# Two shared down products moved behind the turns of the last two dense tiles

## The chip, the cores and the metric

The kernel runs on one core of one Trainium2 chip. Its time is the device time of one execution in microseconds; the time before is the median of three runs. One further execution was recorded by the hardware profiler; all durations below come from it.

The engines are called by their profile names: PE is TensorE (matrix products), PEld its weight loads, DVE is VectorE, ACT is ScalarE, POOL is GpSimd and SP is SyncE. They run at the same time and wait for each other through semaphores; each works through its own instructions in order.

## The reference, cut to what matters

The input is eight batches of 256 rows with 512 columns. The model adds a cross attention to x, and then a mixture of experts:

```python
x = x + xattn(layernorm(x), ctx, mask, Wq, bq, Wk, bk, Wv, bv)
flat = layernorm(x)                      # 2048 tokens of 512
g = flat @ shared_gate.T                 # 352 wide
u = flat @ shared_up.T
shared_out = sigmoid(g) * u @ shared_down.T          # float32
weights = softmax(flat @ router_w.T)                 # 8 experts
comb = the two largest weights of each token, 0 elsewhere
he = sigmoid(xb @ wg) * (xb @ wu)        # bfloat16, each expert
routed = sum over experts of comb * (he @ wd)
x = x + layernorm(x) + shared_out + routed
```

What is computed for a token therefore has a shared part (float32) and the part of its two experts (bfloat16).

## The kernel before, in words

**Attention first.** The first three quarters of the span and more are the attention of the eight batches, head by head. The change does not touch it.

**The tokens of all but the last half batch are sorted by expert.** They go through the experts in `NT` = 37 tiles of 128 rows, whose results are scattered to DRAM (`zs`) and read back later. The last half batch (batch 7, rows 128 to 255) can't be sorted in time. Its 128 tokens go through all eight experts, one tile for each: these are the *dense tiles*, numbers 37 to 44. Their results are summed in one PSUM bank called `sum`.

**Three steps for each tile**, made by `stream`:
- `gate_up_of(t)` (L820): gate product `eg` and up product `eu`, four matmuls each; ScalarE takes the tanh (L825), VectorE multiplies it into h, the tile `hz` (L826).
- `turn_h(t)`: h is turned by three matmuls into the bank `pht` (L836 for a dense tile, where the weight of the expert is multiplied in by a diagonal matrix); for a dense tile ScalarE copies it to SBUF as `hT` (L841).
- `down_of(t)` (L849): three matmuls of hT with the down weights; a dense tile's go to `sum`.

The stream is software-pipelined: after `gate_up_of(t)` stand `down_of(t-2)` and `turn_h(t-1)`. So a gate and up product usually stands between the turn of a tile and its down product. At the stream's end there are no more tiles to put there; its last five steps are down 42, turn 43, down 43, turn 44 and down 44.

**The shared part of the last batch** comes from `shared_units(B - 1, False)`: 24 fine steps (gate and up, L940; h by L952 and L964) and six down products (L998), each a float32 product of 128 columns of h with 512 columns of `sdT`, three chunks for each half of the batch. The chunks of the second half (`tt` = 1, elements 27 to 29 of the list) go into the bank `sum`, on top of the dense tiles' results. Those of the first half (`tt` = 0, elements 24 to 26) go into a bank `psy`, behind two matmuls (L997) that merge the expert results of that half. VectorE then adds the residual: L1012 for `sum`, with the output on SyncE's queue (L1016); L1007 for `psy`, in two parts of 256 columns, with outputs on the queues of SyncE and ScalarE (L1010).

**The order at the end is written out by hand.** The list `todo` (L1303) is gone through in order, and each step issues its instructions at once. `by(n, steps)` makes one step of n. Between the steps the loop issues `adds`: VectorE's additions of read-back expert results to the other halves (L917), each pair followed by its output on SyncE's queue (L919). `done` sums the steps' costs, an addition is issued when `done` passes `due`, and all that are left are issued from some step near the end on.

Of the kernel before, what the change touches and what calls it, by code (L numbers as in the profile page):

```python
# [36 lines left out]
def xattn_ffn_kernel(  # L37
# [840 lines left out]
    def give_back():  # L878


        halves = [(b, tt) for b in range(B) for tt in range(2)][:NS]
        room = deque(
            [four.tile([P, T], F32, tag=tag, name="again") for tag in "qk" for _ in range(3)]
        )
        for _ in range(3):
            e = three.tile([P, 2, T], F32, tag="e", name="again2")
            room.extend(e[:, i, :] for i in range(2))
        byrow = zs.rearrange("(r c) t -> r c t", c=2)
        Z = []

        def rooms(pool, tag, n, tiles=1):

            for _ in range(tiles):
                z = pool.tile([P, n, 2, T], BF16, tag=tag, name="z_" + tag)
                Z.extend(z[:, j] for j in range(n))

        def all_rooms():
            rooms(two, "V", 3, 2)
            rooms(three, "extra", 1, 3)
            rooms(two, "xT", 2)  # L900
            rooms(two, "x", 2)
            rooms(five, "acc", 1)
            rooms(one, "O", 1)

        def again(b, tt):
            S[b]["acc", tt] = a = room.popleft()
            nc.gpsimd.dma_start(out=a, in_=ACC[b][tt])

        def results(n):
            if not Z:  # L910
                all_rooms()
            nc.sync.dma_start(out=Z[n], in_=byrow[n * P : (n + 1) * P])

        def add(n, c):
            b, tt = halves[n]
            a = S[b]["acc", tt]
            nc.vector.tensor_add(a, a, Z[n][:, c, :])  # L917
            if c == 1:
                nc.sync.dma_start(out=out[b, tt * P : (tt + 1) * P, :], in_=a)  # L919

        n = range(NS)
        return (
            deque(lambda of=of: again(*of) for of in halves[: 2 * (NB - 1)]),
            deque(lambda i=i: results(i) for i in n), deque(lambda i=i, c=c: add(i, c) for i in n[:-1] for c in range(2)),
            lambda c: Z[NS - 1][:, c, :],
        )
# [257 lines left out]
    for b in range(B):  # L1184
# [15 lines left out]
        elif b == B - 1:  # L1200
# [5 lines left out]
            fetch, whom, experts, weighted, tiles = expert_tiles()  # L1206
# [57 lines left out]
    tiles, units = deque(tiles), deque(units)  # L1264
# [21 lines left out]
    again, results, adds, own_results = give_back()  # L1286
    n = 2
    while n <= NT:
# [7 lines left out]
    todo = shared_units(B - 1, False)  # L1296
    by = lambda n, todo: [
        (sum(us for us, _ in todo[i : i + n]), lambda fs=todo[i : i + n]: [f() for _, f in fs])
        for i in range(0, len(todo), n)
    ]  # L1300

    tiles = list(tiles)
    todo = tiles[:3] + by(4, todo[:24]) + tiles[3:] + by(3, todo[27:]) + by(3, todo[24:27])  # L1303
    done, due = 0.0, 7.0
    ring.remove(0)
    for i, (us, go) in enumerate(todo):
        go()
        done += us
        if i == 0:
            while results:  # L1310
                results.popleft()()
        while adds and (done > due or i >= len(todo) - 3):
            due += 0.5 if i < 9 else 1.0
            adds.popleft()()

# [32 lines left out]
```

## Time and profile before

| | us |
|---|---|
| median of three runs | 870.91 (870.66 to 870.98) |
| the profiled execution, whole time | 869.63 |
| its span | 867.8 |
| PE busy | 826.3 (95%) |
| DVE busy | 580.8 (67%) |
| turn of tile 43, its first matmul | starts 855.16 |
| last product into `psy`, end | 864.15 |

The page of the profile gives the busy time of each engine and its share of the span. The chain of waits follows the work that ended last back to its releasers; each of its rows has a start in us from the span's start, a length, and an engine with a tile and a line, and "xN" is the number of instructions in the row. "issue" is time for which the profile shows no cause; a row of DVEq or ACTq is that engine's hand-over. A timeline row has start, length, engine, line, operation, output<-inputs, shapes, and in brackets the idle time before it with what ended it. A length of several matmuls overlaps with the next row's, as matmuls are pipelined and their ends are modelled.

### The profile page before, as it was taken

Reading aid. Unit: us, or ns where it says so; the run is one execution under the profiler, and the core shown is the slowest. Engines: PE = TensorE matmul, PEld = TensorE weight load, DVE = VectorE, ACT = ScalarE, POOL = GpSimd, SP = SyncE. Lnnn points to the kernel's source line nnn. Section 1 sums busy time; section 2 is a strip of 40 time slices with the busy share of each in tenths; the row PEclk is TensorE's granted clock in tenths of the full one; section 3 lists DMA queues with packets and bytes.
Section 4 is the critical chain, followed back from the end, with each engine's and each line's share of the span. In section 5 each row is a group of like instructions: output and inputs, shape, how many; then the busy total and the mean of one; then the engine's idle time right before and its main releaser. Section 6 shows DMA issues by size and latency. Waiting matters only on the chain.

```text
span 867.8 us, 13410 instructions
## 1 busy us (share of the span) xinstructions
PE 826.3 (95%) x4987; PEld 340.0 (39%) x4987; DVE 580.8 (67%) x1106; ACT 365.6 (42%) x478; POOL 312.6 (36%) x380
## 2 busy tenths in 40 slices
PE   7988989999999999999999999999999989899997
PEld 4322323333333334333433343433343333455573
DVE  7666767776777677867676778676766674543347
ACT  4234444343344334433443343434343445256632
POOL 3114303543354345343525151605251223155520
PEclk9999999999999999999999999999999999999999
DMA  4107962231551257115712350011000000267556
GB/s 159 46 33 239 342 192 78 34 45 43 128 100 30 41 123 122 23 36 123 128 22 42 90 99 1 26 34 52 1 25 13 13 13 25 61 147 170 150 169 242
DMA packets 91973, 75.05 MB, mean 86 GB/s; under 512 B 60321, under 2 KB 77756, under 8 KB 91526
## 3 DMA queue, kind: packets, MB, share of 16 engines
q1 hardware_dynamic: 85302, 53.84, 22.8%
q0 software_dynamic: 5904, 19.70, 10.8%
q8 instruction: 40, 0.66, 0.3%
q10 hardware_dynamic: 704, 0.66, 0.2%
q14 instruction: 23, 0.19, 0.1%
HBM read 37.84 MB, written 40.79 MB: 91 GB/s over the span
## 4 chain that ended last, share of the span: by engine, by line
PE 74%; DVE 19%; issue 3%; POOL 2%; ACT 1%; DMA 0%; DVEq 0%; ACTq 0%; POOLq 0%
PE s L436 24%; DVE nm L438 10%; PE av L474 9%; PE psy L998 5%; PE pu L940 4%; PE psq L411 3%; PE psk L411 3%; PE ey L849 3%; PE eu L820 3%; PE eg L820 3%; PE pgu L940 3%; PE pg L940 3%; DVE q L418 2%; PE s L459 2%; PE psv L378 2%
## 5 line engine op out<-in xcount | busy, mean ns | idle before, releaser
L461 ACT ACTIVATE e<-s 128x1024 f32<-128x1024 f32 x256 | 262.0, 1023 | 398.5 <-PE s L459 396.6
L438 DVE TENSOR_REDUCE nm<-s 128x2 f32<-128x1024 f32 x256 | 313.3, 1224 | 144.4 <-PE s L459 131.3
L436 PE MATMUL s<-k,q 32*128 32x512 f32 x1024 | 287.7, 639 | 25.3 <-DVE nm L438 22.7
L459 PE MATMUL s<-q,k 32*128 32x512 f32 x1024 | 288.5, 640 | 1.5 <-DVE q L448 0.8
L474 PE MATMUL av<-e,V 128*32 128x512 f32 x1024 | 137.4, 605 | 0.2 <-ACT e L461 0.2
L436 PEld LDWEIGHTS s<-k,q 32*128 32x128 f32 x1024 | 76.6, 183 | 130.2 <-DVE nm L438 104.7
L401 POOL TENSOR_SCALAR extra<-mb,alpha,beta 128x512 f32<-128x512 f32 x60 | 45.5, 763 | 146.1 <-DVE q L418 145.7
L343 POOL TENSOR_TENSOR rs<-ve,mhalf 128x1 f32<-128x1 f32 x32 | 18.4, 575 | 217.0 <-DVE ve L341 216.9
L459 PEld LDWEIGHTS s<-q,k 32*128 32x128 f32 x1024 | 76.5, 182 | 5.3 <-issue 4.3
L474 PEld LDWEIGHTS av<-e,V 128*32 128x32 f32 x1024 | 20.3, 108 | 98.2 <-issue 96.3
L195 POOL DMA_INDIRECT xs<-xnb,at x30 | 30.2, 1006 | 73.9 <-DVE at L669 59.3
L826 DVE SCALAR_TENSOR_TENSOR hz<-eth,eu 128x352 bf16<-128x352 f32 x45 | 23.4, 520 | 41.6 <-ACT eth L825 18.2
L998 PE MATMUL psy<-sdT,h 128*128 128x512 f32 (+1 forms) x90 | 45.3, 615 | 0.2 <-issue 0.2
L940 PE MATMUL pu<-xT,sguT 128*128 128x256 f32 x128 | 36.7, 403 | 0.0
L940 PE MATMUL pg<-xT,sguT 128*128 128x256 f32 x128 | 35.3, 401 | 0.0
L378 PE MATMUL psv<-WvT,ctx 128*128 128x256 f32 x128 | 34.8, 394 | 0.0
L940 PE MATMUL pgu<-xT,sguT 128*96 128x256 f32 (+1 forms) x128 | 34.1, 393 | 0.0
L820 PEld LDWEIGHTS <-late_ctx 128*128 128x128 bf16 x296 | 27.6, 98 | 14.0 <-issue 2.6
L411 PE MATMUL psq<-xm,WqT 128*128 128x512 f32 x64 | 32.0, 620 | 0.9 <-DVE xm L1103 0.9
L195 POOL DMA_INDIRECT whose<-who,at x30 | 29.0, 968 | 9.1 <-issue 9.1
L940 PEld LDWEIGHTS pu<-xT,sguT 128*128 128x128 f32 x128 | 21.8, 189 | 25.3 <-issue 22.8
L411 PE MATMUL psk<-ctx,WkT 128*128 128x512 f32 x64 | 31.6, 617 | 0.0
(219 smaller groups left out, 980.4 us busy)
## 6 DMA issues: line engine op xcount, KB each, us to landing
xs<-blank SPq DMA_DIRECT2D x7, 1920.0 KB
x<-in_x_dram SPq DMA_DIRECT2D x7, 512.0 KB
ctx<-in_ctx_dram SPq DMA_DIRECT2D x7, 512.0 KB
accd<-acc SPq DMA_DIRECT2D x12, 256.0 KB
again<-accd POOLq DMA_DIRECT2D x12, 256.0 KB
out_dram<-again SPq DMA_DIRECT2D x12, 256.0 KB
gu<-in_L_ffn_w_gate_dram POOLq DMA_DIRECT2D x8, 352.0 KB
gu<-in_L_ffn_w_up_dram POOLq DMA_DIRECT2D x8, 352.0 KB
```

What stands on the lines that cost most here:

```text
L195: i = nc.gpsimd.indirect_dma_start(to[:, :], bass.IndirectOffsetOnAxis(ap=rows, axis=0), what, None, **bounds).ins
L378: nc.tensor.matmul(ps, ct[:, kc, sc * P : (sc + 1) * P], WvT[:, kc, :], start=(kc == 0), stop=(kc == 1))
L401: engine.tensor_scalar(t, S[b]["mb"], at, be, ALU.mult, ALU.add)
L411: nc.tensor.matmul(ps, W[:, kc, g // 2].rearrange("p j a d -> p (j a d)"), rhs[:, kc, :], start=(kc == 0), stop=(kc == 1),)
L436: nc.tensor.matmul(ps[:, jj, :], q[r, tci * P : (tci + 1) * P], k[r, :], start=True, stop=True)
L438: best = lambda: nc.vector.reduce_max(NM[G % 2][:, tci, c0 : c0 + 33 : 32], ps, axis=AX.X)
L459: nc.tensor.matmul(ps[:, jj, :], k[r, sc * P : (sc + 1) * P], q[r, :], start=True, stop=True)
L461: nc.scalar.activation(e, ps, AF.Exp)
L474: nc.tensor.matmul(AVT[G][32 * j : 32 * j + 32, :], V[:, sc, 2 * g + j // 2, j % 2 : j % 2 + 2, :].rearrange("p o d -> p (o d)"), et[j // ...
L820: nc.tensor.matmul(ps, xT[:, kc, :], weights_of(t, GU, I, (m * NKC + kc) * I), start=(kc == 0), stop=(kc == NKC - 1),)
L940: lambda kc=kc: nc.tensor.matmul(ps, sguT[:, m, kc, i0 : i0 + n + more], s["xT"][:, kc, :], start=(kc == 0), stop=(kc == NKC - 1))
L998: nc.tensor.matmul(t["y"], t["h"][:n, ic, tt * P : (tt + 1) * P], sdT[:n, ic, :], start=(ic == 0 and b < B - 1), stop=(ic == 2),)
```

## The change

The three products of the second half no longer stand together behind the stream. The first stands between the turn of tile 43 and its down product, the second between the turn of tile 44 and its down product, and the third behind the last down product, where all three stood. All three remain in the bank `sum`, which is read after the third. They are now three single steps instead of one, so the list has two steps more, and the loop's rule for the remaining additions counts four steps from the end instead of three.

```diff
     tiles = list(tiles)
-    todo = tiles[:3] + by(4, todo[:24]) + tiles[3:] + by(3, todo[27:]) + by(3, todo[24:27])
+
+    todo = (
+        tiles[:3] + by(4, todo[:24]) + tiles[3:-3] + todo[27:28] + tiles[-3:-1] + todo[28:29] + tiles[-1:]
+        + todo[29:] + by(3, todo[24:27])
+    )
     done, due = 0.0, 7.0
     ring.remove(0)
     for i, (us, go) in enumerate(todo):
@@
-        while adds and (done > due or i >= len(todo) - 3):
+        while adds and (done > due or i >= len(todo) - 4):
             due += 0.5 if i < 9 else 1.0
             adds.popleft()()
```

## The prediction

> **What bounds the kernel now.** I read the page first, then the chain of waits for the last 90 us, then the timelines of single engines over the last 15 us, because the change touches nothing earlier. The page says that TensorE is the busy engine over the whole span, at the full granted clock in every slice:
>
> ```profile
> PE 826.3 (95%) x4987; PEld 340.0 (39%) x4987; DVE 580.8 (67%) x1106; ACT 365.6 (42%) x478; POOL 312.6 (36%) x380
> PEclk9999999999999999999999999999999999999999
> ```
>
> That average says nothing of the last 13 us. The chain that ended last, in order of time (start, length, what), does:
>
> ```profile
> 854.68 0.65 PE sum L849 x3
> 855.33 0.18 PE pht L836 x3
> 855.51 0.02 issue
> 855.53 0.02 ACTq L841
> 855.54 0.04 issue
> 855.58 0.49 ACT hT L841
> 856.07 0.05 issue
> 856.12 0.82 PE sum L849 x3
> 856.94 0.18 PE pht L836 x3
> ...
> 857.73 0.82 PE sum L849 x3
> 858.55 2.58 PE sum L998 x6
> 861.13 0.43 PE psy L997 x2
> 861.56 2.59 PE psy L998 x6
> 864.15 0.02 issue
> 864.18 0.42 DVE acc L1007
> ```
>
> Read it so. Tile 42's down product (sum L849) still runs straight on from the work before it and costs 0.65 us for three matmuls. Behind it tile 43's h is turned (pht, 855.33) and TensorE has nothing else to do: it stands until ScalarE has copied the turned h to hT. The copy is on the path (0.49 us and 0.13 us of hand-over around it). Its down product then costs 0.82 instead of 0.65 us, since the first matmul behind a standstill also shows its own fill. The same happens once more with tile 44 (856.94 to 858.55). Then come the shared down products of the last half batch, three into the bank `sum` (858.55, two records for each float32 product, 2.58 / 3 = 0.86 us per product), two merging matmuls, three products into `psy`, and VectorE's last multiply-add. So in the tail TensorE sets the end, and two standstills on ScalarE's copy lie on that path.
>
> Two other engines could take the end over. VectorE's timeline:
>
> ```profile
> 856.07 0.52 DVE L826 SCALAR_TENSOR_TENSOR hz<-eth,eu 128x352 bf16<-128x352 f32 x1
> ...
> 859.76 1.41 DVE L917 TENSOR_TENSOR acc<-acc,z_acc 128x512 f32<-128x512 f32 x2
> 861.17 0.69 DVE L1012 SCALAR_TENSOR_TENSOR acc<-sum,acc 128x512 f32<-128x512 f32 x1
> 864.18 0.76 DVE L1007 SCALAR_TENSOR_TENSOR acc<-psy,acc 128x256 f32<-128x256 f32 x2 [2.32 <-PE psy L998]
> ```
>
> VectorE is full of adds until 861.17, takes `sum` there, is done at 861.86 and then idles 2.32 us for TensorE. SyncE's queue:
>
> ```profile
> 861.89 0.33 SPq L1016 DMA_DIRECT2D out_dram<-acc  x1
> 864.63 0.33 SPq L1010 DMA_DIRECT2D out_dram<-acc  x1
> ```
>
> The output of the half taken from `sum` is issued at 861.89; its data move from about 862.0 to 863.5 by the DMA view of these last us. The last output's data move from 865.2.
>
> **The change, part by part.** It removes no instruction and adds none: the built order has the same 4186 TensorE instructions, two products of L998 standing earlier, and on VectorE, ScalarE, GpSimd and SyncE the same order with the same waits. So the adds, although their rule (`done > due`, and the flush at the end) was touched, stay in the same order, and no DMA is moved past any other. Nothing queues behind a new wait: the weight load of hT already waits for ScalarE; it now has a product ahead of it.
>
> *First product, between tile 43's turn and its down product.* In place of the standstill TensorE runs 0.86 us, from 855.51 to 856.37. Meanwhile ScalarE copies as before: it is released by the turn's last matmul, which stands ahead of the product in both orders, so hT is ready at 856.12, 0.25 us before the product ends. Tile 43's down product then follows without standing: 0.65 us, to 857.02.
>
> *Second product, between tile 44's turn and its down product.* The turn costs 0.17, to 857.19; its h (hz) is on VectorE until 856.07 + 0.52 = 856.59, so it is in time by 0.4 us. Product to 858.05; hT ready at 857.19 + 0.61 = 857.80, again 0.25 us early; down product 0.65, to 858.70.
>
> *What is left.* One product into `sum` 0.86, to 859.56; the merging matmuls 0.43; three products 2.58: TensorE ends at 862.57 instead of 864.15. The saving is 1.58 us. Crosscheck from the other side: each standstill is 0.61 us plus the 0.17 us of the slower first matmul, 0.78; twice, 1.56.
>
> *What the two insertions may cost.* Each puts a float32 weight load straight behind a matmul of 128 columns and again a bfloat16 load behind float32 work. The second kind is free in the trace: the merging pair's bfloat16 loads lie under float32 matmuls (860.54 against a matmul that ends later) and that pair costs its plain 0.43. For the first kind the nearest row is the end of tile 38's turn:
>
> ```profile
> 834.47 0.33 PE L836 MATMUL pht<-diag,hz 128*128 128x128 bf16 x3
> 834.63 0.62 PE L940 MATMUL pgu<-xT,sguT 128*96 128x256 f32 x2
> ```
>
> Three turns start at 834.47 and the float32 matmul starts 0.16 us later, so no stall shows at its start; in the chain the sixteen matmuls of that group take 3.48 against 3.45 and 3.47 of the two groups behind it, so 0.00 to 0.03 us. [...] The row agrees that these loads are slow: 190 ns at L998 against 98 ns for bfloat16. If the load had to be complete before its matmul starts, all but the 57 ns of the turn's last matmul (0.17 / 3) would be bare, 0.13 us at each place, and the saving would be 1.58 - 0.27 = 1.31. [...] The row gives 1.52 to 1.58. I take 0.015 us each, by the row, since it is the same transition in the same queue, and keep 0 and 0.27 as ends: saving 1.55.
>
> *Where the stall goes.* Nothing new is late on TensorE. At the end, VectorE's last multiply-add can start at 862.60; VectorE is free from 861.86, so 0.74 us of cover is left there (it was 2.32). If VectorE were late by more than that, the saving would shrink by the excess. `sum` is complete at 859.56 instead of 861.13, but VectorE takes it at 861.17 as before, behind its adds: that earlier readiness is worth nothing. The last output is issued at about 863.07, when SyncE is past L1016 (862.22), and its data would move from 863.65, just behind the other half's, which end at 863.5; should they overlap, the bound is the rest of 128 KB, about 0.35 us at the 386 GB/s shown there. I count 0 for it.
>
> *Sum.* Profiled execution: 869.63 us, 867.8 of span and 1.8 around it; less 1.55 gives a span of about 866.25 and 868.1 us. The median of the runs shown is 870.91, 1.28 above that execution. Only the tail moves, so the difference carries over: 870.91 - 1.55 = 869.36, a saving of 0.18%.
>
> **The rivals.**
>
> *The wait stays, only behind the product.* If ScalarE saw the turn only when the product had passed (or hT's weight load couldn't go ahead during it), each standstill would still come after the 0.86 us, and the time would be 870.9 to 871.0 (with 0.06 for transitions). Against it: tiles 40 to 42 do the same thing with gate products in place of the shared one, and there ScalarE starts its copy while TensorE runs on (849.50, 851.57, 853.58, each with the copy at 0.48 us and no idle time ahead of the next down product). One covered and one bare would give 870.1.
>
> *The end passes to VectorE or to the output.* If the adds slipped by 1.5 us, the last multiply-add would start at 863.4 and the saving would be about 0.8: 870.1. For it: the adds read results that arrive late in the same stretch. Against it: no wait for data stands in that part of VectorE's timeline.
>
> *Slower than before.* The stretch from 855.5 to 862.6 becomes seven us of TensorE without a pause, two thirds of it float32. If the granted clock fell there, its 7.06 us would stretch. At half the clock that is 7.06 more, net 5.5 slower: 876.4. To end 0.2% slower it must eat 1.55 + 1.74 = 3.3 us, which needs a clock of 7.06 / 10.36 = 0.68. Against it: 834.80 to 845.20 is ten us of unbroken float32 at a granted clock of 1.00.
>
> *A little more than reckoned.* Two bfloat16 groups may start better than their steady 0.65, or runs scatter in its favour; beyond 1.74 us it counts as faster.
>
> **How the numbers follow.** About 0.2% (1.74 us) is what a measurement of this kernel can tell from no change, and my saving lies just inside. Full saving as worked out: 0.80; wait stays in full or half: 0.09; end passes to another engine: 0.06; slower clock: 0.05. Of the first, saving 1.55 with ends 1.31 and 1.6 and a scatter of some tenths between medians (the three runs differ by 0.32), about three in eight would be read beyond 1.74: 0.30 faster. Same takes the rest of it, 0.50, and both middle cases but 0.01: 0.64. Slower: 0.06. Range: low 868.4, which is nearly the profiled execution's own basis (868.1), since a set of runs may lie as low as that one did; high 870.6, which takes in half the saving and a scatter of 0.5. The likeliest case alone is 869.1 to 869.7.
>
> **What would show it.** In the changed profile: two records of L998 on `sum` directly behind each of the last two turns; no wait of TensorE for ScalarE's hT there, and down products of 0.65 us; ScalarE's copies at about 855.6 and 857.25; the last `psy` product ending near 862.6; VectorE's idle time ahead of L1007 down from 2.32 to about 0.75. Wrong would be: a wait for hT that remains behind the product, float32 loads that stand bare by over 0.1 us, VectorE ending its adds later than 861.2, or the last output landing less than 1.5 us earlier though TensorE ended so.

## The result and the profile after

The changed kernel's median is 869.01 us (867.94 to 869.90, 11 runs) against 870.91 (869.33 to 872.91, 11 runs); the ratio is 0.9977 with a 95% interval of 0.9967 to 0.9986. In a second comparison, on one chip, it was 869.43 us (22 runs) against 871.26 (61 runs), ratio 0.9982, interval 0.9972 to 0.9992. The ratios are not the quotients of the medians (869.43 / 871.26 is 0.9979). The first is 0.23% faster, the second 0.18%, which is the forecast; both intervals hold both values, so on which side of 0.2% the change lies is not settled.

The profiled execution of the changed kernel took 869.90 us with a span of 868.1, no less than the 867.8 of before. It came to the tail later, so spans say nothing here, and the tail has to be read for itself. This is its chain of waits, in order of time (start, length, what):

```profile
856.44 0.65 PE sum L849 x3
857.09 0.17 PE pht L836 x3
857.26 0.91 PE sum L998 x2
858.17 0.65 PE sum L849 x3
858.82 0.17 PE pht L836 x3
858.99 0.91 PE sum L998 x2
859.90 0.65 PE sum L849 x3
860.55 0.86 PE sum L998 x2
861.41 0.43 PE psy L997 x2
861.84 2.59 PE psy L998 x6
864.43 0.02 issue
864.46 0.42 DVE acc L1007
```

Both rows of ScalarE's copy have gone from the chain. Each turn (pht) is followed at once by a float32 product into `sum`, and the down products behind them are back at 0.65 us. The copies themselves still take their time, under the products. ScalarE's timeline:

```profile
857.35 0.48 ACT L841 CAST hT<-pht 128x384 bf16<-128x384 f32 x1 [1.00 <-PE pht L836]
859.08 0.48 ACT L841 CAST hT<-pht 128x384 bf16<-128x384 f32 x1 [1.25 <-PE pht L836]
```

VectorE's and TensorE's timelines, the rows that answer to those of before:

```profile
861.52 1.41 DVE L917 TENSOR_TENSOR acc<-acc,z_acc 128x512 f32<-128x512 f32 x2
862.84 0.69 DVE L1012 SCALAR_TENSOR_TENSOR acc<-sum,acc 128x512 f32<-128x512 f32 x1
864.46 0.75 DVE L1007 SCALAR_TENSOR_TENSOR acc<-psy,acc 128x256 f32<-128x256 f32 x2 [0.93 <-PE psy L998]
```

```profile
856.93 0.33 PE L836 MATMUL pht<-diag,hz 128*128 128x128 bf16 x3
857.09 1.08 PE L998 MATMUL sum<-sdT,h 128*128 128x512 f32 x2
858.01 0.81 PE L849 MATMUL sum<-dT,hT 128*128 128x512 bf16 x3
```

Before, the same stretch of TensorE's timeline was:

```profile
855.16 0.33 PE L836 MATMUL pht<-diag,hz 128*128 128x128 bf16 x3
856.12 0.82 PE L849 MATMUL sum<-dT,hT 128*128 128x512 bf16 x3 [0.63 <-ACT hT L841]
```

From the first matmul of tile 43's turn to the end of the last `psy` product it is 864.43 - 856.93 = 7.50 us, where it was 864.15 - 855.16 = 8.99: 1.49 less. From there to the end of the span it is 3.67 us, as before (3.65). VectorE's idle time before its last multiply-add has fallen from 2.32 to 0.93 us, so TensorE still sets the end.

### The profile page after: what moved, and what is told of

It is laid out like the page before. It is cut to its first block, busy times and chain, and to the rows that moved or that the text cites. A ratio compares the mean times of both kernels' runs of the same rounds, so it can differ in the third digit from the quotient of the medians.

```text
span 868.1 us, 13410 instructions
## 1 busy us (share of the span) xinstructions
PE 828.3 (95%) x4987; PEld 341.3 (39%) x4987; DVE 580.7 (67%) x1106; ACT 365.7 (42%) x478; POOL 312.9 (36%) x380
## 4 chain that ended last, share of the span: by engine, by line
PE 74%; DVE 19%; issue 3%; POOL 2%; ACT 1%; DMA 0%; DVEq 0%; ACTq 0%; POOLq 0%
PE s L436 24%; DVE nm L438 10%; PE av L474 9%; PE psy L998 5%; PE pu L940 4%; PE psq L411 4%; PE psk L411 3%; PE ey L849 3%; PE eu L820 3%; PE eg L820 3%; PE pgu L940 3%; DVE q L418 2%; PE s L459 2%; PE pg L940 2%; PE psv L378 2%
```

## Experiments

Each is an edit of the changed kernel. "Tail" is the time from the first matmul of tile 42's down product to the end of the last `psy` product: 9.64 us before, 8.15 after. It is read in each trace, because totals scatter by more than these edits move.

### One product only

```diff
-        tiles[:3] + by(4, todo[:24]) + tiles[3:-3] + todo[27:28] + tiles[-3:-1] + todo[28:29] + tiles[-1:]
-        + todo[29:] + by(3, todo[24:27])
+        tiles[:3] + by(4, todo[:24]) + tiles[3:-3] + todo[27:28] + tiles[-3:]
+        + todo[28:] + by(3, todo[24:27])
```

> Only the first product is moved, behind the turn of tile 43; the second stands behind the last down product again. I measure the tail from the first matmul of tile 42's down product to the end of the last product into psy: 9.64 us before, 8.15 after. If each product covers its own standstill for itself, half the saving: 8.90 (9.64 - 0.78 + 0.05 for the slower float32 start), and tile 44's standstill of 0.78 is back. If one product in the stream were enough to bring ScalarE ahead for both tiles, 8.15.

One execution: 869.34 us, against 870.74 for one of before. Its timeline on TensorE:

```profile
855.61 0.33 PE L836 MATMUL pht<-diag,hz 128*128 128x128 bf16 x3
855.77 1.08 PE L998 MATMUL sum<-sdT,h 128*128 128x512 f32 x2
856.69 0.81 PE L849 MATMUL sum<-dT,hT 128*128 128x512 bf16 x3
857.34 0.33 PE L836 MATMUL pht<-diag,hz 128*128 128x128 bf16 x3
858.29 0.82 PE L849 MATMUL sum<-dT,hT 128*128 128x512 bf16 x3 [0.63 <-ACT hT L841]
```

Tile 43 goes through without standing, tile 44 stands as before. The last product ends at 863.86. The first record of the down product is missing in this trace, so I count from the turn: 863.86 - 855.61 = 8.25, plus the 0.65 of the down product is 8.90, as expected. The saving is the sum of two independent halves: 0.74 us here, 1.49 with both.

### Both products in front of the turns

```diff
-        tiles[:3] + by(4, todo[:24]) + tiles[3:-3] + todo[27:28] + tiles[-3:-1] + todo[28:29] + tiles[-1:]
+        tiles[:3] + by(4, todo[:24]) + tiles[3:-4] + todo[27:28] + tiles[-4:-2] + todo[28:29] + tiles[-2:]
```

> Both products are moved into the stream, but each in front of a turn (of tiles 43 and 44) in place of behind it. Theory, cover: nothing runs while ScalarE copies, both standstills stay, tail 9.64 as before. Rival, that the split of the group or the earlier completion of the bank sum brings the gain: 8.15. It also tells what the 0.05 us are that a float32 product took more behind a turn (0.91 against 0.86): behind a down product of 512 columns the weight load is covered, so 0.86 each and tail 9.64 if the bare load is the cause; 0.91 each and tail 9.74 if every change from bfloat16 to float32 costs it.

One execution: 872.87 us. Its chain of waits:

```profile
858.57 0.86 PE sum L998 x2
859.42 0.18 PE pht L836 x3
...
859.69 0.49 ACT hT L841
860.17 0.05 issue
860.22 0.82 PE sum L849 x3
861.04 0.86 PE sum L998 x2
861.90 0.18 PE pht L836 x3
...
862.16 0.49 ACT hT L841
```

Both copies are on the path again. The tail is 9.64 within the reading (the first down record is missing here too: 867.40, less the product's start at 858.40, plus 0.65 is 9.65). So neither the split nor an earlier filling of the bank brings anything; the place behind the turn does. The products take 0.86 here, not 0.91, so not every change from bfloat16 to float32 costs the 0.05. The weight loads of this run and of the changed kernel differ in how early they begin:

```profile
858.19 0.41 PEld L998 LDWEIGHTS sum<-sdT,h 128*128 128x128 f32 x2
```

```profile
857.04 0.30 PEld L998 LDWEIGHTS sum<-sdT,h 128*128 128x128 f32 x2
```

Behind the 512 columns of a down product the load begins 0.21 us ahead of its matmul (858.40). Behind the turn's 128 columns (second fence) it begins only 0.05 us ahead (857.09). That matmul still starts in time, 0.16 us after the turn's first; it is longer. The changed kernel's first float32 matmul, and the first one of the row that the prediction used (in the profile of before), each alone:

```profile
857.09 0.65 PE L998 MATMUL sum<-sdT,h 128*128 128x512 f32 x1
```

```profile
834.63 0.41 PE L940 MATMUL pgu<-xT,sguT 128*96 128x256 f32 x1
```

The one behind it takes 0.59 in the first case and 0.38 in the second. To the nanosecond, the first is longer by 56 ns with a load of 190 ns, and by 29 ns with one of 163 ns (96 columns): in both cases the load's length less 134 ns. Two cases fit; no run varied the load alone.

The total of this execution lies above before's though the tail is the same; the granted clock of its first 50 us was 0.93, and that is taken up in the last section.

### Half a product in each gap

Only the first product is moved, cut in two by columns; the second and third stand together behind the last down product.

```diff
-        tiles[:3] + by(4, todo[:24]) + tiles[3:-3] + todo[27:28] + tiles[-3:-1] + todo[28:29] + tiles[-1:]
-        + todo[29:] + by(3, todo[24:27])
+        tiles[:3] + by(4, todo[:24]) + tiles[3:-3] + [(0.43, lambda: down_part(0))] + tiles[-3:-1]
+        + [(0.43, lambda: down_part(1))] + tiles[-1:] + todo[28:] + by(3, todo[24:27])
     )
+    down_part = lambda i: M["down"](1, 0, i)
```

(Not shown: `down` takes a third argument here, which half of the columns it makes.)

> Too little cover: only the first product is moved, cut into two halves of 256 columns, one behind each of the two turns. Theory: from the first matmul of the turn to the first of the down product ScalarE's copy sets 0.96 us (855.16 to 856.12 before), whatever TensorE does in it, so 0.96 stays, each half saves its 0.43 and its slower start is hidden too: tail 9.64 - 0.86 = 8.78. Rival, that a queued product delays the release of the copy or of the weight load behind it: interval of 1.1 or more, tail 9.0 or more.

One execution: 870.07 us. TensorE's timeline at the first turn:

```profile
856.45 0.33 PE L836 MATMUL pht<-diag,hz 128*128 128x128 bf16 x3
856.62 0.65 PE L999 MATMUL sum<-sdT,h 128*128 128x256 f32 x2
857.41 0.82 PE L849 MATMUL sum<-dT,hT 128*128 128x512 bf16 x3
```

From turn to down product it is 0.96 us, and 0.95 at the second turn (858.07 to 859.02), the same as with an empty gap (855.16 to 856.12), and the tail is 864.59 - 856.45 + 0.65 = 8.79 against 8.78 expected. So in these runs the hand-over through ScalarE took 0.95 to 0.96 us from turn to down product, empty or with a half in it; the two halves saved 9.64 - 8.79 = 0.85 us, which is one product's length (0.86), so their slower start cost nothing. With a whole product in the gap it is 1.08 (856.93 to 858.01 in the changed kernel).

### A third gap

In the profile of before TensorE also waited once for VectorE, whose h of tile 40 stood behind additions in its queue (848.56 to 849.08; the turn began at 849.13, 0.25 us after it could have, 848.23 + 0.65). The timeline of before:

```profile
848.23 0.81 PE L849 MATMUL sum<-dT,hT 128*128 128x512 bf16 x3
849.13 0.34 PE L836 MATMUL pht<-diag,hz 128*128 128x128 bf16 x3
849.30 0.76 PE L820 MATMUL eg<-guT,late_xm 128*128 128x352 bf16 x4
```

Here the three products stand in three gaps, the first in front of the turn of tile 40; the multiply-add of `sum` stays behind the last down product, which now closes the bank. (Not shown: the edits of `down` and `down_of` for this.)

```diff
+        tiles[:3] + by(4, todo[:24]) + tiles[3:8] + [(0.0, todo[27][1])] + tiles[8:-3] + todo[28:29] + tiles[-3:-1]
+        + [(0.86, lambda: M["down"](1, 2, "product"))] + tiles[-1:]
+        + [(0.0, lambda: M["down"](1, 2, "end"))] + by(3, todo[24:27])
```

> All three products stand in gaps: the first in front of the turn of tile 40, where TensorE waits for VectorE's h behind its additions (0.42 us lost at 848.88 to 849.47 before), the second and third behind the turns of tiles 43 and 44; the last down product closes the bank. Measured from the first matmul of tile 39's down product to the end of the last psy product: 15.92 before, 14.43 after. If that wait is covered like the others: 14.01. If VectorE's queue only hands the delay on to a later h: 14.4. VectorE's idle time ahead of L1007, 0.93 after the change, should shrink to about 0.5.

One execution: 867.86 us. TensorE's timeline:

```profile
848.23 0.81 PE L849 MATMUL sum<-dT,hT 128*128 128x512 bf16 x3
848.88 1.02 PE L1001 MATMUL sum<-sdT,h 128*128 128x512 f32 x2
849.74 0.33 PE L836 MATMUL pht<-diag,hz 128*128 128x128 bf16 x3
849.91 0.76 PE L820 MATMUL eg<-guT,late_xm 128*128 128x352 bf16 x4
```

The last product ends at 862.41, so the stretch is 14.18 us, not 14.01 and not 14.43. The wait is covered, but it was worth 0.25, not 0.42: I had read it off the chain, where the turn behind it is 0.34 long, and had counted the other 0.17 as lost too. From the turn's start to the next gate product it is 0.17 with the wait and without it (849.13 to 849.30, 849.74 to 849.91). VectorE's idle time before its last multiply-add (L1010 in this kernel) is 0.65; about 0.5 was expected.

The same kernel against before, 22 runs:

> All three products in gaps, timed. Its trace shows the tail (from tile 39's down product on) at 14.18 against 15.92 before and 14.43 after, so 1.74 less than before: ratio 0.9980, 0.25 us under the changed kernel. If only totals of the kind seen in the looks count (867.86 against 870.74), ratio 0.9967.

Median 869.14 us, ratio 0.9973, interval 0.9963 to 0.9982; it takes in 0.9980. Its interval overlaps that of the changed kernel (0.9972 to 0.9992), so the 0.25 us between them are shown by the trace alone.

### The last half's end split

The `psy` group is made in two halves of 256 columns, in two banks, each with its own multiply-add and output behind it. This stands on top of the three gaps. (Not shown: the list, in which two steps of `last_half` take the place of the last one, and the rule for the additions, which counts five.)

```diff
+        def last_half(i):
+            cols = slice(i * T // 2, (i + 1) * T // 2)
+            y = bank([P, T], F32, "psy", own)[:, : T // 2]
+            for c in range(2):
+                nc.tensor.matmul(y, twice, own_results(c)[:, cols], start=(c == 0), stop=False)
+            for ic, (i0, n) in enumerate(ICH):
+                nc.tensor.matmul(y, t["h"][:n, ic, :P], sdT[:n, ic, cols], start=False, stop=(ic == 2))
+            acc = s["acc", 0]
+            nc.vector.scalar_tensor_tensor(acc[:, cols], y, 0.5, acc[:, cols], ALU.mult, ALU.add)
+            (nc.sync, nc.scalar)[i].dma_start(out=out[b, :P, cols], in_=acc[:, cols])
```

> As the kernel with three gaps, and the last product group is made in two halves of 256 columns in two banks, so that VectorE's first half and its output are done while TensorE makes the second. Theory: from the last psy product to the end of the span 3.3 us in place of 3.65, as L1007's second half no longer stands behind its first; the last product itself at most 0.1 later through the additional weight loads; ratio 0.9976. Rival, that VectorE is now the bound (0.65 us idle were left): its multiply-add of sum ends about 861.8, the first half follows at once, and the second half waits for it: gain under 0.1. Second rival, that both outputs collide with the output issued before: end of span still 3.6 behind the last product.

VectorE's timeline:

```profile
861.86 0.68 DVE L1012 SCALAR_TENSOR_TENSOR acc<-sum,acc 128x512 f32<-128x512 f32 x1
862.46 0.41 DVE L1026 SCALAR_TENSOR_TENSOR acc<-psy,acc 128x256 f32<-128x256 f32 x1
863.23 0.42 DVE L1026 SCALAR_TENSOR_TENSOR acc<-psy,acc 128x256 f32<-128x256 f32 x1 [0.36 <-PE psy L1024]
```

The second half waits for TensorE, not for VectorE. From the last product (863.21) to the end of the span (866.5) it is 3.29 us in place of 3.69 in the kernel with three gaps (862.41 to 866.1), and from the turn of tile 43 to the last product 6.68 in place of 6.65. So the trace gives 0.37 us, and no delay of one output by the other shows in it (3.3 us was expected without one, 3.6 with). The median is 868.64 us, ratio 0.9977 with 0.9963 to 0.9991: faster than before, but not told apart from the changed kernel by its total.

### The rule for the additions alone, and the changed kernel again

```diff
-        tiles[:3] + by(4, todo[:24]) + tiles[3:-3] + todo[27:28] + tiles[-3:-1] + todo[28:29] + tiles[-1:]
-        + todo[29:] + by(3, todo[24:27])
+        tiles[:3] + by(4, todo[:24]) + tiles[3:]
+        + todo[27:] + by(3, todo[24:27])
```

> The other part of the change alone: the three products stand together behind the last down product as before, as three steps, with the rule of four steps for the additions. All engines' orders are those of before. Tail 9.64 us as before, ratio 1.000; it also shows how far two kernels with the same order lie apart in such a comparison (0.2% at most is my estimate, from the spread of the runs before).

> The changed kernel once more, beside before and the other three on one chip. In the trace its tail is 1.49 us shorter, while the first medians lie 1.90 apart. If the tail is all, the medians differ by 1.5, ratio 0.9983, and what lay above that was the scatter of the early part (100 us into the span, where the profile shows stretches at a lower granted clock in some executions). If the change also acts elsewhere, again 1.9 or more, ratio 0.9978 or less.

The rule alone: 871.18 us, ratio 1.0000 (0.9986 to 1.0013); from the turn of tile 43 to the last product 868.78 - 859.79 = 8.99 us, as before. The changed kernel again: 862.26 - 854.75 = 7.51 us there. By its ratio it saved 0.18% or 1.57 us, with an interval of 0.70 to 2.44, which is as the tail alone would have it; but its median still lies 1.83 us under that of before. So the totals do not tell the tail's 1.49 us from the 1.90 of the first medians. That the change acts in the tail alone rests on the traces: the order of instructions up to there is the same, and the last section shows where executions part.

## Why the prediction was right

It gave 869.36 us with a range of 868.4 to 870.6; 869.01 was measured. By its steps:

- *TensorE sets the end, and two standstills on ScalarE's copy lie on its path:* right. Both went, and each brought its own half (one product only: 8.90 us of tail; both in front of the turns: 9.65). One label in it is loose: the down product behind a standstill does not itself cost 0.82. By starts it takes 0.65 there too (856.12 to 856.77). What a standstill costs is 0.96 us from turn to down product less the 0.17 of a covered turn, 0.79, which is the prediction's 0.61 + 0.17. The copy begins behind the end of the turn's last matmul (855.58, after 855.16 + 0.33 = 855.49), while the product of the changed kernel begins ahead of that end (857.09, with 856.93 + 0.33 = 857.26). The wait for VectorE's h of tile 40 stood in front of the turn and not behind it, so there the 0.17 was not lost (849.13 to 849.30).
- *The copy runs on under the product and is ready 0.25 us early:* right. ScalarE's copy ended at 857.83, the product at 858.17; with the hand-over of 0.05 that is 0.29 early.
- *The price of the slower start:* wrong in size. I took 0.015 us each, from the start of the gate and up group; it was 0.05 each (0.91 against 0.86). That row shows no late start, but its first matmul is 0.03 longer (0.41 against 0.38), which is the upper end of the 0.00 to 0.03 that I read from the chain; and its loads have 96 columns, not 128, so it was not the same transition. For the two places together it is 0.10, between the prediction's ends of 0 and 0.27, and 1.58 - 0.10 = 1.48 is near the 1.49 that came. The upper end, with the load complete before its matmul starts, is not what the trace after shows: the first load stands there from 857.04 to 857.23 (190 ns), its matmul begins at 857.09, and the matmul is longer by 56 ns, not by 190 - 57 = 133.
- *VectorE does not take over:* right. 0.93 us of cover were left, 0.74 were forecast; its additions did not slip. Half of the difference is the smaller saving (2.32 - 1.49 = 0.83). The rest is a term that I put at nothing, the earlier readiness of `sum`: before, its multiply-add began 1.41 us after the last pair of additions (859.76 to 861.17), just behind the end of the third product at 861.13; in the changed kernel 1.32 after (861.52 to 862.84), which is the pairs' own pace (858.44 to 859.76 in before).
- *The output does not collide:* right, 3.67 us from the last product to the end against 3.65.
- *The difference carries over to the median:* not contradicted. The second comparison gave a ratio of 0.9982, the forecast 0.18%, the first one 0.9977; but the medians lie 1.90 and 1.83 us apart, and the second interval reaches from 0.70 to 2.44 us. That 869.01 lies within 0.4 us of the forecast is therefore luck in part.

Of the rivals, the wait that stays behind the product and VectorE as the new bound are refuted by the trace after. A slower clock over the last seven us did not occur: the granted clock from 856 to 868 us was 1.00 in the trace after.

## What to carry to other kernels

At the end of a software pipeline the steps that used to cover each other's hand-over run out, and work from another group can take their place, if it does not need what is being handed over and its result is read later (here both kinds of product add to `sum`, which is read when all have been added). Reckon the gain of a filler by the measured start-to-start time of the hand-over (0.96 us here), and place it behind the instruction that starts the hand-over: the same products in front of it brought nothing (9.65 us of tail against 9.64). Where the effect is below the scatter of totals, read the stretch in the trace and use totals only as a check.

## What the runs showed of the hardware

The tail is the same to 0.01 us in every trace of an order (8.99 and 8.99; 7.50 and 7.51), but the time at which the same instruction order reaches it is not: the first matmul of tile 43's turn stood at 854.75, 855.16, 856.93 and 859.79 us in four of them, although up to there they issue the same instructions (VectorE's 1106 instructions stand in the same order in all four). Two places are visible.

The first is a stretch at a lower clock. The busy times by stretch (from and to in us of the span, length, the five engines, granted clock, DMA), in before and in the changed kernel's first profile:

```profile
50.00:60.00 10.00, 8.58 (x61) 2.97 (x59) 6.10 (x7) 3.60 (x4) 0.00 (x0) 1.00 0.19 67
```

```profile
50.00:60.00 10.00, 8.89 (x53) 3.00 (x51) 5.38 (x7) 2.50 (x3) 0.00 (x0) 0.83 0.05 15
52.50:55.50 3.00, 3.00 (x15) 0.79 (x12) 1.23 (x1) 1.02 (x1) 0.00 (x0) 0.50 0.02 5
```

In slices of half a microsecond the clock is 0.50 from about 52.3 to 55.7 us and 1.00 around it. That is 3.4 us at half the clock, a loss of 1.7 us by my estimate if TensorE is busy all the time. The rule alone had the same stretch; both products in front of the turns had 0.50 from about 33.2 to 40.1 us, twice as long, and ran 3.25 us behind before from there to the tail.

The second is one small product on VectorE (L598). In before and in the rule alone, and what GpSimd did beside it in the latter:

```profile
430.40 0.18 DVE L598 TENSOR_TENSOR w<-w,m 128x16 f32<-128x16 f32 x1
```

```profile
433.62 1.70 DVE L598 TENSOR_TENSOR w<-w,m 128x16 f32<-128x16 f32 x1
433.78 1.51 POOL L401 TENSOR_SCALAR extra<-mb,alpha,beta 128x512 f32<-128x512 f32 x2
```

The same 128x16 product took 0.18 us in one and 1.70 in the other, until GpSimd's two instructions ended (435.32 and 435.29), and TensorE then waited 1.37 us for VectorE. In before it began 0.17 us ahead of GpSimd's, here 0.16 ahead. In the rule alone this happened twice where before had 0.18 (342.69 and 433.62, 1.44 us later each time); in the changed kernel's first profile once, for 0.97 us, up to the end of the first of GpSimd's two (431.41 to 432.38; that one ended at 432.33), 0.72 later. This and the early part, at whose end (72 us) the rule alone was 1.8 us and the changed kernel 1.0 us behind before, make up the lag at the turn of tile 43: 1.8 + 1.44 + 1.44 for the 4.63 us of the rule alone, 1.0 + 0.7 for the 1.77 of the changed kernel. That GpSimd holds VectorE up was not shown: no run moved the one from the other. At other places of before the times coincide again (519.89 to 521.71, GpSimd's to 521.70) and once not (160.64 to 162.18, GpSimd's two to 161.82).

Sorted by the mean clock of the execution, the medians at 1.000 are 869.65 us for before (23 runs), 868.40 for the change (8), 868.03 with three gaps (5), 867.74 with the split end (6), 869.93 for the rule alone (4); before at 0.998 is 871.7 (15). By them the change is worth 1.25 us. Executions of one kernel thus differ by more than the change brings. What makes the clock fall in some executions was not tried.
